# The third layer's first loads on GpSimd's queue, the offsets' filters first, and the attention's pools in another order

## The chip, the cores and the metric

The kernel runs on one core of one Trainium2 chip. A core has five engines that each work through their own list of instructions in order and wait for each other by semaphores: TensorE (PE in the profile, its weight loads PEld), VectorE (DVE), ScalarE (ACT), GpSimd (POOL) and SyncE (SP), which here only issues loads and stores. The metric is the time of one execution on the device in microseconds, as the median of several runs.

## The reference

The network takes `x` of shape (2, 256, 64, 64), two images of 256 channels, and puts four layers behind each other, all in float32:

- Layer 0: group norm, then attention with 4 heads of 64 channels over the 4096 pixels, a projection, and the normalized input added.
- Layer 1: a position term (a linear function of the pixel's row and column) is added.
- Layer 2: a bottleneck. A 1x1 convolution to 64 channels, a deformable 3x3 convolution with a mask, a 1x1 convolution back to 256, batch norms and the input added.
- Layer 3: twice group norm, ReLU and a deformable 3x3 convolution on 256 channels, and the input added at the end.

The part that matters here is the deformable convolution of layer 3:

```python
f = lax.conv_general_dilated(x, dw, (1, 1), 'SAME', feature_group_count=C, dimension_numbers=dn)
off = lax.conv_general_dilated(f, pw, (1, 1), 'SAME', dimension_numbers=dn)
off = (off + pwb[None, :, None, None]) * OFFSET_SCALE
...
sampled = bilinear_gather(x, py, px)
out = jnp.einsum('bckhw,ock->bohw', sampled, w.reshape(O, C, KK))
```

`dw` is a 7x7 filter per channel, `pw` a 1x1 convolution to 18 channels (nine taps, two coordinates). Each output pixel reads the image at nine shifted places by bilinear interpolation, four pixels for each, and the nine samples are multiplied with `w`.

## The kernel before

`Net.run` calls `attention` (layers 0 and 1, and as background work most of layer 2) and then `deform` (what is left of layer 2, and layer 3). In both, PE, ACT, DVE and POOL are put under `manual_schedule`, and SP is left out of it. What counts for this document is the order in which the instructions stand on each engine in the built program.

**Attention** goes through four units (two images, two pairs of heads), each with 16 blocks of 256 queries. For a block, PE makes scores (L533), DVE takes the largest (L542), ACT the exponentials (L549), PE turns them (L561), ACT and DVE copy them out (L576, L578), and PE multiplies with the values into `av` (L588). When a block is done, `weights` and `spread` send the softmax shares through a small table in device memory (L464) and back as `f` (L468). `combine` multiplies and adds on POOL: `o` times `f` (L474), halves added (L475), and the result written to `avs` (L480). Every second block, `project` multiplies `avs` with `wproj` on PE (L498), and DVE adds it to `res` (L508). `res` goes to device memory (L510), and `second_layer` makes the first 1x1 convolution of layer 2 from it (L840).

**Layer 2** has a class of its own, `Bottleneck`. After L840, ACT writes `h` (L850), PE transposes it (L865), DVE copies it to `imgt` (L869), and SP stores it as an image in device memory (L874). `offsets` of this class makes the offsets on PE (L883, L904), and `corners` turns them into row numbers `bidx` and weights on DVE (L671 to L709). `conv` gathers `bfour` tiles from the stored image by indirect DMA on POOL (L766), two gathers to a tile; DVE multiplies them with the weights and adds them (L947, L956, L957: `bsmp`), and PE multiplies on (L967, L976). In `deform`, `conv` of the second image uses a ring of nine `bfour` tiles (the call is `bott.pools(inner, 9)`), gathers eight tiles ahead, and is stepped along beside layer 3.

**Layer 3**, in `deform`, starts with loads on SP: four pieces of 1 MB of the first image `x` from `xn` (L1113), where the background of attention put it long before, nine tiles `wc` of the convolution's weights (L1145), and `dw` and `pw` of the offsets (L1124, L1126). DVE multiplies `dw` and `pw` into the combined filter `wf` (L1131). For each of 8 blocks of 512 pixels, 14 products on PE make `pd` from `x` and `wf` (L726; each is two records in the profile), ACT copies it to `wide` (L737), PE sums shifted copies (L743), ACT adds the bias (L752), PE transposes (L757) and `corners` makes `didx` and the weights. The main loop then gathers `four` (L766, 128 rows of 1024 numbers), weighs the four corners on ACT (L1239) and DVE (L1245) into `smp`, transposes on PE (L1257), copies to `st` on ACT (L1266) and multiplies with `wc` (L1276). `Side` objects step other work along at a fixed rate per pass: the offsets of the coming blocks, the rest of layer 2, and the images of the next layer. Ahead of the main loop, 58 passes (L1337 and on) step only the first offsets and, every third time, layer 2's `conv`.

**Places in memory.** Tiles lie in pools, and pools are stacked in the order in which they are opened. When `attention` ends, its pools are given up, and `deform`'s pools take the same places from the start on. The first instruction that writes into a pool of `deform` waits for all earlier readers and writers of the places that this pool covers. Before, attention opens `att_w`, `att_work`, `att_one`, `att_x`, `att_q`, `att_k`, `att_v`, `att_e`, `att_et` in this order; `att_one` holds `o`, `f`, `avs`, `res` and `pos`. `deform` first opens `df_w`, which holds `x` of the first image (32 KB of each partition), `dw`, `pw`, `wf`, `wide` and `wc`.

Of the kernel before, what the change touches and what calls it, by code (L numbers as in the profile page):

```python
# [9 lines left out]
F32 = mybir.dt.float32  # L10
# [8 lines left out]
P = 128  # L19
B, C, H, W = 2, 256, 64, 64  # L20
# [5 lines left out]
DWK = 7  # L26
# [12 lines left out]
class Net:  # L39
# [108 lines left out]
    def attention(self, bott):  # L148
# [4 lines left out]
        tc, nc, a = self.tc, self.nc, self.a  # L153
        with ExitStack() as ctx:
            wp = ctx.enter_context(tc.tile_pool(name="att_w", bufs=1))
            work = ctx.enter_context(tc.tile_pool(name="att_work", bufs=2))
            one = ctx.enter_context(tc.tile_pool(name="att_one", bufs=1))
            xp = ctx.enter_context(tc.tile_pool(name="att_x", bufs=4))
            qp = ctx.enter_context(tc.tile_pool(name="att_q", bufs=2))
            kp = ctx.enter_context(tc.tile_pool(name="att_k", bufs=5))  # L160
            vp = ctx.enter_context(tc.tile_pool(name="att_v", bufs=6))
            ep = ctx.enter_context(tc.tile_pool(name="att_e", bufs=4))
            etp = ctx.enter_context(tc.tile_pool(name="att_et", bufs=2))
            bt = bott.pools(ctx)
            psc = ctx.enter_context(tc.tile_pool(name="att_sc", bufs=2, space=PSUM))
            ptp = ctx.enter_context(tc.tile_pool(name="att_tt", bufs=2, space=PSUM))
# [30 lines left out]
            for i in range(NB):  # L197
                t = xp.tile([P, 2, 512], F32, name="xb") if i < 4 else rest[:, i - 4]
# [8 lines left out]
            gmask = wp.tile([P, P], F32, name="gmask")  # L207
            nc.sync.dma_start(gmask, a["gmask"][:, 0, :])
            nc.sync.dma_start(wqkv, a["wqkv"])
            wproj = wp.tile([P, 2, C], F32, name="wproj")  # L210
            self.later.append((wproj, a["wproj"]))

            units = [(b, hp) for b in range(B) for hp in range(2)]
# [407 lines left out]
            n = 0  # L621
# [453 lines left out]
    def deform(self, bott):  # L1075
# [4 lines left out]
        tc, nc, a = self.tc, self.nc, self.a  # L1080
        with ExitStack() as ctx:
            wp = ctx.enter_context(tc.tile_pool(name="df_w", bufs=1))
            work = ctx.enter_context(tc.tile_pool(name="df_work", bufs=2))
# [22 lines left out]
            x, stats = {}, dict(bott.stats)  # L1106

            def load(b, src, pool):
                x[b] = pool.tile([P, 2, HW], F32, name=f"x{b}")
                src = src.rearrange("(cb p) n -> p cb n", p=P)  # L1110
                for i in range(4):
                    cols = slice(1024 * i, 1024 * i + 1024)
                    nc.sync.dma_start(x[b][:, :, cols], src[:, :, cols])  # L1113

            load(0, self.xn_d[0], wp)
            ods = [wp.tile([P, 8, W + DWK - 1], F32, name=f"wide{n}") for n in range(2)]
            for t in ods:
                nc.gpsimd.memset(t, 0.0)
            base = bott.base

            def offset_weights(l):

                dw = wp.tile([P, 2, T], F32, name="dw")
                nc.sync.dma_start(dw, a["dw"][l])  # L1124
                pw = wp.tile([P, 2, 2 * K2], F32, name="pw")
                nc.sync.dma_start(pw, a["pw"][l])  # L1126
                yield
                yield
                self.wf = wp.tile([P, 2, T, 2 * K2], F32, name="wf")
                for cb in range(2):  # L1130
                    nc.vector.tensor_tensor(  # L1131
                        self.wf[:, cb],
                        dw[:, cb].unsqueeze(2).to_broadcast([P, T, 2 * K2]),
                        pw[:, cb].unsqueeze(1).to_broadcast([P, T, 2 * K2]),
                        ALU.mult,
                    )
                    yield
# [9 lines left out]
            def image(b, l):  # L1147

                if l == 0:
                    load(b, self.x2d[b], ctx.enter_context(tc.tile_pool(name="df_x1", bufs=1)))  # L1150
# [39 lines left out]
            def offsets(b, l):  # L1190
                if b == 0:
                    yield from offset_weights(l)
                wf = self.wf
                for i in range(NB):
                    idx = cp.tile([P, 4, K2], I32, name="didx")
                    w4 = cp.tile([P, 4, K2, 4], F32, name="dw4")
                    corners[b, l, i] = idx, w4
                    yield from self.offsets(
                        i,
                        [x[b][:, cb, :] for cb in range(2)],  # L1200
                        lambda s, row: wf[:, s, DWK * row : DWK * row + DWK, :].rearrange(
                            "p t o -> p (t o)"
                        ),
                        self.vec[:, V_PWB + l : V_PWB + l + 1],
                        base, idx, w4, work, ods, pd,
                    )

            layers = [(b, l) for l in range(2) for b in range(B)]
            BLOCK = 4 * K2
            LAYER, ALL = NB * BLOCK, len(layers) * NB * BLOCK  # L1210
            AHEAD, LEAD = 8, BLOCK + 16
# [119 lines left out]
            OFFS = 24  # L1331
            inner = ExitStack()
            second = bott.conv(1, bott.pools(inner, 9), ps)
            offs = [Side(-LEAD - 6, OFFS / BLOCK, offsets(0, 0))]
            for k in range(K2):
                conv_weight(0, k)
            for s in range(-LEAD - 6, 0):  # L1337
# [10 lines left out]
            for s in range(ALL + 12):  # L1348
                n = s // LAYER
# [22 lines left out]
                if s % LAYER == LAYER - LEAD - 8 and n + 1 < len(layers):  # L1372
                    for o in images + offs:
                        for _ in o.steps or ():
                            pass
                    images, offs = [], []
                    offs.append(Side(s, OFFS / BLOCK, offsets(*layers[n + 1])))
# [97 lines left out]
```

## Time and profile before

| what | value |
|---|---|
| median of 3 timed runs | 5586.81 us (5586.36 to 5594.37) |
| the profiled execution | 5402.33 us |
| its span, first to last instruction | 5400.6 us |
| mean granted clock of TensorE | 0.967 |
| PE, DVE, ACT, POOL busy | 92%, 79%, 54%, 38% of the span |
| last `av` product of attention ends | 3136.7 us |
| first product of the third layer's offsets | 3182.0 us |
| first `four` gather of the third layer | 3212.4 us |

The profile is one execution, recorded by the hardware; it was 184.5 us shorter than the median of the timed runs. A line of a chain gives the start, the length in microseconds, and the piece of work that the next one waited for. A line of a timeline gives start, length, engine, source line, operation, what it writes and reads, how often, and in brackets how long its engine sat idle before and what ended that. A line of the stretches gives, for each engine, the busy time and the number of instructions, then the granted clock of TensorE as a share of full speed, the share of time that the 16 DMA engines were busy, and GB/s. Records of SP and of loads are times of issue; when a load has landed is told by what waited for it.

### The profile page before, as it was taken

To read this page: it belongs to the slowest core of one execution; us is meant where nothing else is said; L and a number is where in the kernel's file an instruction comes from. 1 tells how busy PE (TensorE), PEld (TensorE's weight loads), DVE (VectorE), ACT (ScalarE), POOL (GpSimd) and SP (SyncE) were. 2 spreads that over 40 slices of the span, in tenths; PEclk is the share of its full clock that TensorE was granted. 3 is DMA by queue.
4 is the path that set the end of the run, shared out by engine and by line. 5 is a ranking of instruction groups with operands and counts; after the bars stand their busy time and mean duration, and the time that the engine had idled before them with its cause. 6 is when DMAs were issued, how large, how long until landed. Compare 5 with 4: busy or idle time off the path is not lost.

```text
span 5400.6 us, 97530 instructions
## 1 busy us (share of the span) xinstructions
PE 4976.3 (92%) x37208; PEld 2665.3 (49%) x37208; DVE 4249.0 (79%) x8066; ACT 2897.7 (54%) x5333; POOL 2068.6 (38%) x1946
## 2 busy tenths in 40 slices
PE   8999999999999999999999977767899999999998
PEld 5555555555555555555555533333444444444443
DVE  6877767787668888677766648787899999999998
ACT  5676656666566666566666622222444444444444
POOL 0111101000024343233200047777566566656665
PEclk9999999999999999999999978888999999999999
DMA  5221111101113222222141146666999999999998
GB/s 168 62 89 58 41 64 39 48 29 44 48 54 89 77 82 90 80 78 74 50 136 34 35 156 231 225 223 231 353 333 330 341 360 358 352 390 353 342 349 320
DMA packets 347363, 920.29 MB, mean 170 GB/s; under 512 B 58972, under 2 KB 98698, under 8 KB 346894
## 3 DMA queue, kind: packets, MB, share of 16 engines
q0 software_dynamic: 193536, 679.59, 35.4%
q1 hardware_dynamic: 153358, 234.46, 13.5%
q8 instruction: 292, 4.78, 0.4%
q14 instruction: 177, 1.45, 0.1%
HBM read 815.90 MB, written 89.60 MB: 168 GB/s over the span
## 4 chain that ended last, share of the span: by engine, by line
PE 65%; DVE 17%; issue 6%; DMA 5%; ACT 5%; POOL 2%; SPq 0%; ACTq 0%; DVEq 0%; POOLq 0%
PE sc L533 14%; PE av L588 14%; PE out L1276 10%; PE tt L561 9%; DVE smp L1245 8%; PE pd L726 5%; DMA four<-img,didx 3%; PE pt L1257 3%; DVE low L542 2%; ACT e L549 2%; PE pm L976 1%; POOL bfour L766 1%; DVE bfour L947 1%; PE pm L498 1%; PE pm L247 1%
## 5 line engine op out<-in xcount | busy, mean ns | idle before, releaser
L1245 DVE SCALAR_TENSOR_TENSOR smp<-four,dw,smp 128x256 f32<-128x256 f32 x3456 | 1611.8, 483 | 168.5 <-ACT smp L1239 85.5
L549 ACT ACTIVATE e<-sc,low 128x1024 f32<-128x1024 f32 x1024 | 1147.5, 1121 | 646.0 <-DVE low L542 645.0
L542 DVE TENSOR_REDUCE low<-sc 128x1 f32<-128x1024 f32 x1024 | 1209.5, 1219 | 295.9 <-PE sc L533 288.2
L766 POOL DMA_INDIRECT four<-img,didx x1152 | 1161.5, 1008 | 656.8 <-DVE smp L1245 307.7
L1276 PE MATMUL out<-st,wc 128*128 128x512 f32 x2304 | 1236.8, 619 | 139.7 <-ACT st L1266 111.3
L533 PE MATMUL sc<-k,qs 64*128 64x512 f32 x2048 | 1029.0, 621 | 7.4 <-ACT e L549 7.1
L533 PE MATMUL sc<-k,q 64*128 64x512 f32 x2048 | 1018.7, 620 | 0.0
L588 PE MATMUL av<-et,v 128*64 128x256 f32 x8192 | 999.1, 386 | 0.0
L561 PEld LDWEIGHTS tt<-ident,e 64*128 64x128 f32 x16384 | 647.9, 140 | 559.1 <-issue 245.0
L474 POOL TENSOR_TENSOR o<-o,f 128x1024 f32<-128x1024 f32 x64 | 153.4, 2396 | 1967.1 <-DVE o L428 1182.8
L766 POOL DMA_INDIRECT bfour<-img,bidx x576 | 579.8, 1007 | 665.6 <-DVE bsmp L957 487.3
L561 PE MATMUL tt<-ident,e 64*128 64x64 f32 x16384 | 751.2, 228 | 86.5 <-ACT et L578 69.4
L578 ACT COPY et<-tt 128x512 f32<-128x512 f32 x1280 | 722.2, 587 | 83.7 <-PE tt L561 80.6
L1239 ACT ACTIVATE smp<-four,dw 128x256 f32<-128x256 f32 x1152 | 524.2, 503 | 430.6 <-DMA four<-img,didx 368.9
L576 DVE COPY et<-tt 128x512 f32<-128x512 f32 x768 | 524.6, 683 | 247.3 <-PE tt L561 245.8
L1257 PEld LDWEIGHTS pt<-ident,smp 128*128 128x128 f32 x2304 | 321.1, 144 | 740.7 <-issue 439.1
L1266 ACT COPY st<-pt 128x1024 f32<-128x1024 f32 x288 | 291.0, 1010 | 721.2 <-PE pt L1257 721.2
L588 PEld LDWEIGHTS av<-et,v 128*64 128x64 f32 x8192 | 544.8, 137 | 257.0 <-issue 1.3
L1276 PEld LDWEIGHTS out<-st,wc 128*128 128x128 f32 x2304 | 393.3, 197 | 402.2 <-issue 207.1
L1257 PE MATMUL pt<-ident,smp 128*128 128x128 f32 x2304 | 457.7, 281 | 67.0 <-DVE smp L1245 61.7
L726 PE MATMUL pd<-x,wf 128*126 128x512 f32 (+2 forms) x896 | 460.8, 601 | 8.4 <-DVE wf L1131 7.3
L533 PEld LDWEIGHTS sc<-k,qs 64*128 64x128 f32 x2048 | 351.2, 192 | 229.7 <-issue 123.6
(153 smaller groups left out, 3369.1 us busy)
## 6 DMA issues: line engine op xcount, KB each, us to landing
f<-share_d SPq DMA_DIRECT2D x128, 256.0 KB, 3.9
xb<-xn SPq DMA_DIRECT2D x55, 512.0 KB, 4.0
img<-imgt SPq DMA_DIRECT2D x96, 256.0 KB, 7.0
four<-img,didx POOLq DMA_INDIRECT x1152, 6.1
xa<-res SPq DMA_DIRECT2D x32, 512.0 KB, 2.7
xb<-in_x SPq DMA_DIRECT2D x20, 512.0 KB, 5.4
bfour<-img,bidx POOLq DMA_INDIRECT x576, 3.0
qs<-q SPq DMA_DIRECT2D x64, 128.0 KB, 4.0
```

What stands on the lines that cost most here:

```text
L533: nc.tensor.matmul(s[:, j, :], lhsT=q[u, i // 2][int(h != j)][halves[j], at : at + P], rhs=k[u][c][halves[j], h, :], start=True, stop=True,)
L542: nc.vector.tensor_reduce(low, s, AX.X, ALU.max, negate=True)
L549: nc.scalar.activation(e.rearrange("p j n -> p (j n)"), s, AF.Exp, bias=blk.low[:, g, c : c + 1], accum_out=blk.sum[:, g, c : c + 1],)
L561: nc.tensor.transpose(pt[:, m, :], e[half, m // 4, m % 4 * P : m % 4 * P + P], self.ident[half, half],)
L576: nc.vector.tensor_copy(dst, pt)
L578: nc.scalar.copy(dst, pt)
L588: nc.tensor.matmul(now["av"][halves[h], :], lhsT=v[u][c][:, m, halves[h]], rhs=ets[j][:, m, h, :], start=(m == 0), stop=(m == 7),)
L726: nc.tensor.matmul(pd[:m, r0 * W : r1 * W], lhsT=wt(s, t), rhs=src[:, (y + r0) * W : (y + r1) * W], start=(n == 0), stop=(n == len(srcs) * ...
L766: self.nc.gpsimd.indirect_dma_start(out=dst, out_offset=None, in_=img, in_offset=bass.IndirectOffsetOnAxis(ap=idx, axis=0),)
L1245: nc.vector.scalar_tensor_tensor(smps[s], four[:, c], weight(s, c), smps[s], ALU.mult, ALU.add)
L1257: nc.tensor.transpose(pts[u][:, c, j * P : (j + 1) * P], smp[:, c * P : c * P + P], self.ident,)
L1276: nc.tensor.matmul(outs[ob], lhsT=wc[k][:, c, ob * P : ob * P + P], rhs=sts[u][:, c, :], start=(k == 0 and c == 0), stop=(k == K2 - 1 and ...
```

## The change

Three things are edited. In `attention`, the pools `att_work` and `att_one` are opened after `att_et` instead of after `att_w`, and `wproj` moves from `att_w` to `att_one`. In `deform`, `dw` and `pw` of the first layer and all pieces of the first image's `x` are issued on GpSimd's queue instead of SP's; those of the second layer and of the second image stay on SP. And the generator of the first offsets is made and stepped once ahead of the load of `x`, so that `dw` and `pw` are issued first; the same generator is handed on to the `Side` that steps it later.

```diff
--- before.py
+++ after.py
@@ -153,14 +153,15 @@
         tc, nc, a = self.tc, self.nc, self.a
         with ExitStack() as ctx:
             wp = ctx.enter_context(tc.tile_pool(name="att_w", bufs=1))
-            work = ctx.enter_context(tc.tile_pool(name="att_work", bufs=2))
-            one = ctx.enter_context(tc.tile_pool(name="att_one", bufs=1))
             xp = ctx.enter_context(tc.tile_pool(name="att_x", bufs=4))
             qp = ctx.enter_context(tc.tile_pool(name="att_q", bufs=2))
             kp = ctx.enter_context(tc.tile_pool(name="att_k", bufs=5))
             vp = ctx.enter_context(tc.tile_pool(name="att_v", bufs=6))
             ep = ctx.enter_context(tc.tile_pool(name="att_e", bufs=4))
             etp = ctx.enter_context(tc.tile_pool(name="att_et", bufs=2))
+
+            work = ctx.enter_context(tc.tile_pool(name="att_work", bufs=2))
+            one = ctx.enter_context(tc.tile_pool(name="att_one", bufs=1))
             bt = bott.pools(ctx)
             psc = ctx.enter_context(tc.tile_pool(name="att_sc", bufs=2, space=PSUM))
             ptp = ctx.enter_context(tc.tile_pool(name="att_tt", bufs=2, space=PSUM))
@@ -207,7 +208,7 @@
             gmask = wp.tile([P, P], F32, name="gmask")
             nc.sync.dma_start(gmask, a["gmask"][:, 0, :])
             nc.sync.dma_start(wqkv, a["wqkv"])
-            wproj = wp.tile([P, 2, C], F32, name="wproj")
+            wproj = one.tile([P, 2, C], F32, name="wproj")
             self.later.append((wproj, a["wproj"]))
 
             units = [(b, hp) for b in range(B) for hp in range(2)]
@@ -1110,20 +1111,18 @@
                 src = src.rearrange("(cb p) n -> p cb n", p=P)
                 for i in range(4):
                     cols = slice(1024 * i, 1024 * i + 1024)
-                    nc.sync.dma_start(x[b][:, :, cols], src[:, :, cols])
-
-            load(0, self.xn_d[0], wp)
-            ods = [wp.tile([P, 8, W + DWK - 1], F32, name=f"wide{n}") for n in range(2)]
-            for t in ods:
-                nc.gpsimd.memset(t, 0.0)
+                    queue = (nc.gpsimd, nc.sync)[b]
+                    queue.dma_start(x[b][:, :, cols], src[:, :, cols])
+
             base = bott.base
 
             def offset_weights(l):
 
+                queue = (nc.gpsimd, nc.sync)[l]
                 dw = wp.tile([P, 2, T], F32, name="dw")
-                nc.sync.dma_start(dw, a["dw"][l])
+                queue.dma_start(dw, a["dw"][l])
                 pw = wp.tile([P, 2, 2 * K2], F32, name="pw")
-                nc.sync.dma_start(pw, a["pw"][l])
+                queue.dma_start(pw, a["pw"][l])
                 yield
                 yield
                 self.wf = wp.tile([P, 2, T, 2 * K2], F32, name="wf")
@@ -1205,6 +1204,13 @@
                         base, idx, w4, work, ods, pd,
                     )
 
+            begun = offsets(0, 0)
+            next(begun)
+            load(0, self.xn_d[0], wp)
+            ods = [wp.tile([P, 8, W + DWK - 1], F32, name=f"wide{n}") for n in range(2)]
+            for t in ods:
+                nc.gpsimd.memset(t, 0.0)
+
             layers = [(b, l) for l in range(2) for b in range(B)]
             BLOCK = 4 * K2
             LAYER, ALL = NB * BLOCK, len(layers) * NB * BLOCK
@@ -1331,7 +1337,7 @@
             OFFS = 24
             inner = ExitStack()
             second = bott.conv(1, bott.pools(inner, 9), ps)
-            offs = [Side(-LEAD - 6, OFFS / BLOCK, offsets(0, 0))]
+            offs = [Side(-LEAD - 6, OFFS / BLOCK, begun)]
             for k in range(K2):
                 conv_weight(0, k)
             for s in range(-LEAD - 6, 0):
```

## The prediction

> **What bounds the kernel now.** I read the page's chain shares first, then the chain in order of time, and looked for where attention ends and the deformable layer begins, since every edit lies there. This is the chain around that place, not its whole length; the columns are start, length (us) and what.
>
> ```profile
> 3149.38 3.69 PE pm L840 x4
> ...
> 3161.71 12.27 DMA wc<-in_dcw
> 3173.98 0.02 issue
> 3174.00 6.83 DMA pw<-in_pw
> 3180.83 0.03 DVEq L1131
> 3180.86 0.04 issue
> 3180.91 1.09 DVE wf L1131
> 3182.00 0.04 issue
> 3182.04 12.90 PE pd L726 x28
> ```
>
> The first product of the offsets (`pd`) starts at 3182.04 because `wf` needs `dw` and `pw`, and SP issued those last, behind four megabytes of `x` and nine `wc`. Next, busy time per stage (PE, PEld, DVE, ACT, POOL, then granted clock, DMA share, GB/s):
>
> ```profile
> 3137.00:3182.00 45.00, 22.96 (x40) 8.83 (x40) 10.42 (x46) 5.58 (x10) 21.36 (x22) 0.55 0.70 245
> 3182.00:3213.00 31.00, 26.92 (x78) 12.32 (x78) 10.44 (x32) 1.87 (x3) 12.88 (x13) 0.94 0.20 59
> ```
>
> For 45 us PE is half idle at half clock; then for 31 us it is busy while POOL waits and DMA idles. Two phases that could overlap stand one after the other. The timeline of POOL shows which wait ends last (start, length, what, idle before and its releaser):
>
> ```profile
> 3139.14 2.34 POOL L474 TENSOR_TENSOR o<-o,f 128x1024 f32<-128x1024 f32 x1 [37.56 <-DMA f<-share_d]
> ...
> 3161.15 0.99 POOL L766 DMA_INDIRECT bfour<-img,bidx  x1 [6.02 <-issue]
> ...
> 3186.09 0.94 POOL L766 DMA_INDIRECT bfour<-img,bidx  x1 [0.30 <-issue]
> 3201.14 0.94 POOL L766 DMA_INDIRECT bfour<-img,bidx  x1 [14.11 <-DVE floor L685]
> ...
> 3212.38 0.94 POOL L766 DMA_INDIRECT four<-img,didx  x1 [0.30 <-issue]
> ```
>
> POOL issues 28 gathers of the second layer, then the first `four`, which opens the third layer's loop. After 20 it stands for 14.11 us: the ring of nine `bfour` tiles is full, and the sums that free it stand on DVE behind `pos<-pd`, which waits for `pd`. So the loop's start is set by the image store (first gather 3161.15) plus 51.2 us of gathers, of which about 15 are a stall that goes back to late `dw` and `pw`. Everything later runs in order behind this.
>
> **What the Trainium skill says.** "DMA: Bandwidth & Descriptors", section "Issuing engines are not separate DMA queues": loads from GpSimd and from SP share the same 16 engines, so moving issues saves sequencer time only. The trace agrees so far as gathers and SP's loads together reach 406 GB/s at 3162 to 3168. Same page, "Anatomy of one DMA — SWDGE (gpsimd) path": about 2.0 us plus bytes/436 GB/s, 4.4 us for 1 MB; no plain load from GpSimd is in this trace. "TensorE: Matmul & The Clock Gate", "What's actually happening": half clock after some 3.4 us idle, full after 3.4 us of work. The trace agrees: granted 1.00 at 3120 to 3137, 0.50 from 3144 to 3182, 1.00 from 3190.
>
> **The change, part by part.** In the changed program's order on each engine, read from the built code:
>
> (a) The pools' order. Before, `df_w` lay over `att_work` and `att_one`, so its first tile waited for the last reader of `res`, the L840 product (3153.06). After, it lies over `att_w`, `att_x`, `att_q`, `att_k` and part of `att_v`, and the wait of `dw` is for the last `av` product (L588), which ends at 3136.7. Head start 16 us. `wproj` moves to `att_one` since L498 reads it late. Within attention only addresses differ and the order is the same: nothing.
>
> (b) POOL now has `dw`, `pw`, `x` piece 1 ahead of the last L474, piece 2 ahead of L475, piece 3 ahead of L480, piece 4 after it. The issue cost of a plain load on POOL is not in this trace. Lower bound SP's 0.37 us (L1113); the nearest POOL row is a gather, 0.95 us plus 0.30 gap for 128 rows; a piece of `x` has 256 runs, so up to twice that. I take 1.0 for `dw` and `pw`, 1.3 for a piece, each plus 0.3. Then `dw` 3136.8, `pw` 3138.1, piece 1 3139.4 to 3140.7, L474 3141.0 instead of 3139.14, and with 1.6 each for two more pieces `avs` is ready at 3149.1 instead of 3143.6: 5.5 us later.
>
> (c) SP, freed of `x`, issues the nine `wc` right after 3136.7 (4 MB less ahead of them). They share the engines with piece 1. At the trace's 380 GB/s some 1.2 of their 2.36 MB are through at 3140.7; sharing alike, piece 1 is in after another 2 MB, 5.3 us, and about 1 us until it counts as landed (an estimate, half of that page's fixed 2.0): 3147. `wf` needs `dw` and `pw` (about 3 us after issue, as a `bfour` gather) and 2.1 us on DVE: 3144, hidden by piece 1. SP then holds the second layer's `dw` until `wf` is done; behind it stand `res`, `xa` and the image store, none of which is due before 3157, so that wait costs nothing (with `wf` later than 3157 it would).
>
> (d) On PE six `pd` products now stand ahead of the first L498, and the other eight between L498, L840, L865 and L883. So attention's tail waits for piece 1: this is what is late next. From 3147: fourteen products took 12.90 us, of which about 2.2 are the cold start (warm, 512 columns take 2 x 0.43). Six are 4.5 warm plus 2.2: 3153.7, when `avs` is long there. But PE is now warm. L498 takes about 1.0 instead of 2.07, L840 1.9 instead of 3.67, and single `pd` fill the waits for DVE (0.70) and ACT (1.08). Stepping through: L498 3153.7, L498 3155.6, L840 3157.4, L865 3160.4, `imgt` copied 3161.4. It was 3155.4: 6.0 us later.
>
> (e) The image store was issued over 2.6 us and the gather followed 3.8 us after the last issue began, with DMA 0.98 busy by `x`. After, `x` and `wc` (6.4 MB from 3137.6 at 380 GB/s) are through by 3155, and the short store's usual landing is 2.2 us, so the first gather comes at 3165.8: 4.6 later than 3161.15.
>
> (f) The 14.11 us stall goes. The remaining `pd` end at about 3168, `pos<-pd` comes at about 3180, and the tile that the 21st gather needs is freed by 3184, while that gather is due at 3191. 28 gathers at 1.25 are 35 us, plus about 2 for those that run beside DVE's sums (1.4 each at 3201 to 3212): 37 instead of 51.2, a gain of 14.2. The memsets of `wide` (1.07 us) stay ahead of the gathers and stay hidden.
>
> Sum: 14.2 - 4.6 = 9.6 us earlier first `four`. Later, the offset products stand one place earlier in the first loop: nothing, PE is 0.72 busy there. Against the profiled execution (5402.33 us, span 5400.6) this is 5392.7. The three timed runs have a median of 5586.81, 184.5 longer; the page does not say where, so I take the same microseconds off: 5577.2. A measurement of this kernel can tell about 0.2%, 11.2 us, from no change.
>
> **Rivals.**
> 1. Cheaper on POOL: a plain load holds POOL no longer than SP, 0.37 us. Piece 1 is issued at 3137.8, lands about 3144.5, and everything from (d) on comes 2.5 us earlier; if the warm PE also saves on the second L883 and L904, the delay is 1 to 2 us and the gain 12 to 14: 5573.5. For: the granted clock of 0.50 through the whole old tail. Against: every POOL DMA in the trace costs 0.95.
> 2. Slower: the tail waits too long for piece 1. The price is one for one from 14.2 us of delay on, and plus 0.2% needs 25.4, so piece 1 landing at about 3168 instead of 3147. The place is the six `pd` ahead of L498 on PE. For: a `wc` under a full queue took 12.27 us to land. Against: even 12.27 us gives 3153 and leaves a gain of 3.6; it would take POOL standing several us on each megabyte. About 5598.
> 3. Given back: the gain is there at 3213, but the loop later loses it. From 3900 on DMA is 0.94 to 0.95 busy at about 349 GB/s, and if what limits there were not the start but heat or another clock state, the end would hardly move: 5586. Against: all of that work is behind the same gathers and starts as much earlier.
> That the loads aren't earlier at all is excluded by the waits in (a).
>
> **How the numbers follow.** The sum as worked out, gain 6 to 11: 0.42. Rival 1: 0.43, since several of my terms are taken high and the ring's stall is fully removed in each case. Rival 3: 0.07. Rival 2: 0.08. Hence faster 0.43, same 0.49, slower 0.08. The predicted time is the sum's, 5577. Its own range is 5575 to 5582 with the unknown POOL issue (gain 5 to 12). For 8 in 10: down to a gain of 17 (no delay of the tail and the spread of the three runs, 8 us, halved), up to a loss of 3: 5570 to 5590.
>
> **What would show it.** Right: `dw` issued by POOL at 3137; `wf` before 3146; the first `pd` before L498, near 3147; L498 near 3154 at about 1 us; first gather at 3164 to 3167; no idle above 2 us between the 28 gathers; first `four` near 3203, and the same distance to the end from there. Wrong: plain loads on POOL of several us; piece 1 after 3152; `imgt` after 3166; a stall of POOL on a `bfour` tile; or a distance from first `four` to the end that differs from 2188 us by more than 3.

## The result, and the profile after

| | before | after |
|---|---|---|
| median of 12 timed runs each | 5587.62 us (5575.4 to 5604.42) | 5581.61 us (5567.48 to 5603.61) |
| ratio, with 95% interval | | 0.9979 [0.9966, 0.9993] |
| the profiled execution, and its span | 5402.33, 5400.6 us | 5603.61, 5601.8 us |
| last `av` product ends | 3136.72 us | 3166.63 us |
| first `four` gather, after that | 75.7 us | 70.0 us |
| from there to the end | 2188.2 us | 2365.2 us |

The kernel is shorter by 6.0 us by the medians, and by 11.7 us (0.21%) by the recorded ratio, which isn't the quotient of the two medians (0.9989); its interval reaches from 0.07 to 0.34%, to both sides of what was named as distinguishable.

The two profiled executions can't be compared as wholes: the kernel before took 5408 us in some sessions and 5588 us in others, once each on chip 14, and the profile of before is of the first kind, that of after of the second. So I count from the end of the last `av` product. Source lines of the changed kernel stand from one lower to six higher (L474 is L475, L498 is L499, L726 is L727, L766 is L767, L1131 is L1130).

The timeline of POOL after answers to the one shown of before (start, length, what, in brackets the idle time before it and what ended it):

```profile
3167.27 0.60 POOL L1123 DMA_DIRECT2D dw<-in_dw  x1 [35.79 <-PE av L589]
...
3168.41 0.74 POOL L1115 DMA_DIRECT2D x<-xn  x1
3169.46 2.33 POOL L475 TENSOR_TENSOR o<-o,f 128x1024 f32<-128x1024 f32 x1 [0.32 <-DMA f<-share_d]
...
3196.59 1.03 POOL L767 DMA_INDIRECT bfour<-img,bidx  x1 [19.24 <-DMA img<-imgt]
...
3228.67 1.15 POOL L767 DMA_INDIRECT bfour<-img,bidx  x1 [4.31 <-DVE bsmp L958]
...
3236.66 0.94 POOL L767 DMA_INDIRECT four<-img,didx  x1 [0.30 <-issue]
```

The loads come straight after the `av` product; the first gather comes 30.0 us after it (24.4 before); and the stall of 14.11 us is a stall of 4.31. PE after, where the chain of before showed `pd` as the last of all:

```profile
3176.45 7.34 PE L727 MATMUL pd<-x,wf 128*126 128x512 f32 x12 [9.82 <-DMA x<-xn]
3183.63 1.02 PE L499 MATMUL pm<-avs,wproj 128*128 128x512 f32 x2
...
3187.34 1.93 PE L841 MATMUL pm<-res,w 128*64 128x512 f32 x4
```

`pd` starts 9.8 us after the last `av` product instead of 45.3, and now attention's tail stands behind it. The stretches (busy us of PE, PEld, DVE, ACT, POOL, then granted clock, DMA share, GB/s), first up to the gathers, then the gathers:

```profile
3166.00:3197.00 31.00, 21.18 (x51) 8.74 (x48) 5.36 (x6) 3.08 (x5) 10.14 (x12) 0.83 0.81 274
3197.00:3237.00 40.00, 24.39 (x76) 10.78 (x74) 15.37 (x71) 4.36 (x8) 27.46 (x29) 0.83 0.38 115
```

Before, it was 45 us at a clock of 0.55 and 31 at 0.94; now PE is busy for 0.68 and 0.61 of the two stretches, at 0.83 in both. What is left of the stall stands behind waits of DVE for which this profile has no releaser ("remote"). Over the whole execution there are 68 such waits of 451 us, nearly all on ACT and DVE, and none in the profile of before:

```profile
3207.99 0.23 DVE L672 TENSOR_TENSOR pos<-pm,base 128x72 f32<-128x72 f32 x1 [4.78 <-remote]
...
3212.23 0.23 DVE L672 TENSOR_TENSOR pos<-pd,base 128x72 f32<-128x72 f32 x1 [3.54 <-remote]
```

### The profile page after: what moved, and what is told of

Its sections match the earlier page's. It is cut to its first block, busy times and chain, and to the rows that moved or that the text cites. A ratio compares the mean times of both kernels' runs of the same rounds, so it can differ in the third digit from the quotient of the medians.

```text
span 5601.8 us, 97517 instructions
## 1 busy us (share of the span) xinstructions
PE 5000.3 (89%) x37208; PEld 2671.1 (48%) x37208; DVE 4247.3 (76%) x8066; ACT 2883.7 (51%) x5333; POOL 2062.6 (37%) x1952
## 5 line engine op out<-in xcount | busy, mean ns | idle before, releaser
L767 POOL DMA_INDIRECT four<-img,didx x1152 | 1153.9, 1002 | 765.5 <-DVE smp L1251 337.8
L475 POOL TENSOR_TENSOR o<-o,f 128x1024 f32<-128x1024 f32 x64 | 153.5, 2399 | 1939.4 <-DVE o L429 1154.3
L767 POOL DMA_INDIRECT bfour<-img,bidx x576 | 577.1, 1002 | 766.3 <-DVE bsmp L958 583.9
L1245 ACT ACTIVATE smp<-four,dw 128x256 f32<-128x256 f32 x1152 | 511.2, 502 | 55.5 <-DMA four<-img,didx 45.9
L727 PE MATMUL pd<-x,wf 128*126 128x512 f32 (+2 forms) x896 | 467.3, 608 | 16.1 <-DMA x<-xn 9.8
```

Of the source, the lines that this page charges most:

```text
L727: nc.tensor.matmul(pd[:m, r0 * W : r1 * W], lhsT=wt(s, t), rhs=src[:, (y + r0) * W : (y + r1) * W], start=(n == 0), stop=(n == len(srcs) * ...
L767: self.nc.gpsimd.indirect_dma_start(out=dst, out_offset=None, in_=img, in_offset=bass.IndirectOffsetOnAxis(ap=idx, axis=0),)
```

## The experiments

My theory is the prediction's: `dw` and `pw`, last in SP's queue, made the stall, and the tail pays a part back by waiting for the first piece of `x`. (The run with the pools' order alone corrects its first half.) The rivals tested: that one part of the change alone gives it, that the queue gives it, that the end doesn't follow the start. "Head" is the time from the end of the last `av` product to the first `four` gather, "rest" from there to the end, both in one profiled execution; "gain" is the difference of the two medians in the same session.

| run | median (before) us | ratio [95%] | gain us | head us | rest us |
|---|---|---|---|---|---|
| e0, before again | 5408.42 (5407.65) | 1.0004 [0.9996, 1.0013] | -0.8 | 75.7 | 2194.6 |
| e1, after again | 5395.14 (5407.65) | 0.9977 [0.9968, 0.9985] | 12.5 | 65.3 | 2189.9 |
| e4, all on SP | 5388.08 (5407.65) | 0.9969 [0.9957, 0.9981] | 19.6 | 59.3 | 2193.6 |
| e6, ring of 11 | 5399.9 (5407.65) | 0.9986 [0.9979, 0.9992] | 7.8 | 71.4 | 2190.7 |
| e2, pools only | 5398.27 (5407.12) | 0.9985 [0.9979, 0.9992] | 8.9 | 74.6 | 2185.8 |
| e3, queue only | 5400.26 (5407.12) | 0.9987 [0.998, 0.9993] | 6.9 | 68.1 | 2194.1 |
| e5, `x` on SP | 5385.58 (5407.12) | 0.9961 [0.9947, 0.9974] | 21.5 | 59.8 | 2189.2 |
| e7, fewer ahead | 5390.67 (5407.12) | 0.9964 [0.9951, 0.9978] | 16.5 | 46.3 | 2203.6 |
| e10, pools only again | 5579.21 (5587.61) | 0.9989 [0.9981, 0.9997] | 8.4 | 75.2 | 2343.3 |
| e11, `x` on SP again | 5570.71 (5587.28) | 0.9958 [0.9945, 0.9972] | 16.6 | 67.3 | 2351.7 |

### Both kernels again, in one session

No edit in e0 (the kernel before) and e1 (the changed kernel).

> The kernel before, unchanged, for a second profile of it. The way from the last av product of attention to the first four gather took 75.7 us in the profile before and 70.0 in the profile after. Theory (the start of the third layer's loop is the image store plus 28 gathers, with a stall of some 14 us on the ring of bfour tiles): 75 to 76 us again, and a stall of 13 to 15 us on POOL in it. Rival (the two profiles differ by the state of the chip and not by the edit): the way varies by several us from one execution to the next, 70 to 80. The span shows as well whether 5400.6 us was an unusual execution: near 5590 if so.

> The changed kernel, unchanged, for a second profile and a narrower interval. Theory: 66 us from the last av product to the first four gather where no engine waits for something that the profile does not show, up to 70 where it does as in the profile after; 8 to 12 us less than before in the timed runs, ratio 0.998. Rival (a gain in the stage that the loop gives back): the same 66 to 70, but a ratio of 1.000.

Neither profile has a "remote" wait, so these two can be compared. The head fell from 75.7 to 65.3 us, 10.4 less; the median by 12.5. Chain of e1 in order of time (start, length, what):

```profile
3142.00 7.59 DMA x<-xn
3149.59 0.14 issue
3149.73 6.87 PE pd L727 x12
3156.60 0.86 PE pm L499 x2
...
3160.22 1.86 PE pm L841 x4
...
3163.89 0.44 DVE imgt L870
...
3166.33 2.21 DMA img<-imgt
```

This is step (d): piece 1 of `x`, six `pd`, then L499, L841 and the image store. The gathers of e1 on POOL:

```profile
3169.41 1.03 POOL L767 DMA_INDIRECT bfour<-img,bidx  x1 [18.82 <-DMA img<-imgt]
...
3205.56 0.94 POOL L767 DMA_INDIRECT four<-img,didx  x1 [0.30 <-issue]
```

28 gathers in 36.2 us, and none of them waits for more than 0.31 us. The rest is 2189.9 us; the unchanged kernel alone showed 2188.2 and 2194.6. So nothing above that scatter was given back.

### The stall by itself: a larger ring

```diff
-            self.ahead = gathers - 1
+            self.ahead = min(gathers - 1, 8)
...
-            second = bott.conv(1, bott.pools(inner, 9), ps)
+            second = bott.conv(1, bott.pools(inner, 11), ps)
```

> The kernel before with a ring of eleven bfour tiles instead of nine in the third layer, still eight tiles ahead; no load is moved. Theory (the stall on the ring sets the loop's start): four more gathers run before the stall, which shrinks by 5 us, so 70 to 71 us from the last av product to the first four gather, and about 5 us less in time. Rival (the late pd product sets it in another way, through didx): the first four stays where it is, 75 to 76 us.

Nothing else of the kernel before is touched; two more tiles take four more gathers before POOL stands. POOL of e6:

```profile
3199.03 0.95 POOL L766 DMA_INDIRECT bfour<-img,bidx  x1 [10.03 <-DVE floor L685]
...
3205.12 1.08 POOL L766 DMA_INDIRECT four<-img,didx  x1 [0.30 <-issue]
```

The stall is 10.0 instead of 14.0 us, the head 4.3 us shorter, the median 7.8 (interval 4.3 to 11.4). The stall on the ring is on the path to the end: less of it, by another means and with all loads as late as before, shortens the kernel. That the median fell by more than the head isn't explained by this, though its interval takes in 4.3.

### The pools' order alone

```diff
-            work = ctx.enter_context(tc.tile_pool(name="att_work", bufs=2))
-            one = ctx.enter_context(tc.tile_pool(name="att_one", bufs=1))
...
+            work = ctx.enter_context(tc.tile_pool(name="att_work", bufs=2))
+            one = ctx.enter_context(tc.tile_pool(name="att_one", bufs=1))
...
-            wproj = wp.tile([P, 2, C], F32, name="wproj")
+            wproj = one.tile([P, 2, C], F32, name="wproj")
```

> Only the pools' order and the place of wproj are changed; all loads stay on SP in the old order (x, then wc, then dw and pw). Times counted from the end of the last av product, beside 17.6 (x), 45.5 (first pd) and 75.7 us (first four gather) of the kernel before. Theory (dw and pw set the start, wherever x stands): x is issued at 0 to 1 us, but dw and pw still stand behind nine wc, so the first pd comes at 30 to 40; the first pos<-pd moves forward by as much, the stall of POOL on the bfour ring shrinks from 14 to about 7 us, and the first four gather comes at 68 to 70: about 7 us less in all. Rival A (the early x is the gain): first four at 60 to 65, 11 us or more. Rival B (early x without early filters is worth nothing): first four at 75 to 76, within 2 us of before.

The head is 74.6 us, rival B. My number for `pd` was wrong (30 to 40; it came at 43.2). This is SP's queue in e2:

```profile
3136.14 1.41 SPq L1114 DMA_DIRECT2D x<-xn  x3
3148.87 0.36 SPq L511 DMA_DIRECT2D xa<-res  x1
3149.27 0.47 SPq L1114 DMA_DIRECT2D x<-xn  x1
...
3157.56 4.91 SPq L1146 DMA_DIRECT2D wc<-in_dcw  x9
3162.51 0.51 SPq L1125 DMA_DIRECT2D dw<-in_dw  x1
```

Three pieces of `x` go at once, but the fourth stands behind the store of `res` in SP's own order, and `dw` behind `wc`, 26.4 us after the last `av` product. That is 10 us earlier than in e0 (36.5), yet `wf` came only 2 us earlier. DVE tells why; first e2, then the kernel before:

```profile
3177.76 0.54 DVE L710 TENSOR_TENSOR bw<-wt 128x36 f32<-128x36 f32 x4
3178.19 2.06 DVE L1132 TENSOR_TENSOR wf<-dw,pw 128x882 f32<-128x882 f32 x2
```

```profile
3178.37 0.54 DVE L709 TENSOR_TENSOR bw<-wt 128x36 f32<-128x36 f32 x4
3180.91 2.07 DVE L1131 TENSOR_TENSOR wf<-dw,pw 128x882 f32<-128x882 f32 x2 [2.00 <-DMA pw<-in_pw]
```

In both, `wf` stands on DVE behind `corners` of the second layer (`bw`), which waits for attention's tail. In e2 `wf` follows it with no idle time: it waited for its place on DVE and for no load, and a stall of 13.89 us stayed. In the kernel before it waited for `pw` only 2.00 us longer. So filters that land earlier are by themselves worth about these 2 us. The rest of the gain goes with the place of `wf`: in the runs that issue the filters first (e1, e3, e4, e5) the built program has it ahead of `corners`, and it starts 2.7 to 21.1 us after the last `av` product instead of 42.1. No run moves `wf` on DVE alone.

Yet the median was 8.9 us less, where the head gives 1.1. Repeated in another session:

> The kernel with the pools' order alone once more, unchanged. If its 8.9 us were scatter, it is now 0 to 4 us less than the kernel before (the first four gather 1.1 us earlier); if they are real, again 6 to 11 us less. In the trace the first four gather should again stand at 74 to 75 us after the last av product, and POOL should again stall for 13.5 to 14.2 us on the bfour ring.

Again 8.4 us less, with a head of 75.2 us and POOL standing for 2.03 and 12.95 us among the gathers. So it isn't scatter of one session, and it doesn't come from the head.

### Attention by itself

In both kernels the call of the deformable part is replaced by a constant that fills the output:

```diff
-            self.deform(bott)
+            for b in range(B):
+                for cb in range(2):
+                    for i in range(HW // P):
+                        dst = self.out[b, P * cb : P * cb + P, P * i : P * i + P]
+                        self.nc.sync.dma_start(dst, self.ident)
```

> The kernel before without its deformable part: after attention the output is filled with a constant, so that only attention and its tail are timed. With its partner below this asks whether the pools' order alters attention itself, since the kernel with the pools' order alone was timed 8.9 us shorter where its trace shows the first four gather only 1.1 us earlier. Theory 1 (attention is the same, the 8.9 us are scatter or lie after attention): the two medians agree within 2 us. Theory 2 (other addresses make attention shorter): the partner is 4 to 8 us shorter.

> The kernel with the pools' order alone, cut in the same way after attention. Theory 1: within 2 us of its partner with the old order. Theory 2: 4 to 8 us shorter.

With the old order 3221.36 us (3215.47 to 3227.69, five runs), with the new one 3217.31 (3210.03 to 3218.91): 4.05 us less by the medians, at a granted clock of 0.976 and 0.979 on average. The ranges overlap, so this doesn't settle theory 2. The two kernels aren't attention alone either: SP issued the 128 stores of the constant in the midst of the first blocks (71 to 147 us), and at 128 us PE sat idle for 13.2 us in e8 and 15.9 us in e9 while they ran. And the profiles of the whole kernel speak against theory 2: in those without a "remote" wait the last `av` product ends at 3133.7 to 3139.3 us with the old order (before, e0, e3, e6) and at 3127.6 to 3142.7 us with the new one (e1, e2, e4, e5, e7), with means of 3136.6 and 3136.3. Between e0 and e2 most of the difference stands in the rest, which differs by 6.4 us between two profiles of the unchanged kernel. So the 8.9 and 8.4 us were timed twice, and where they come from is open.

### The queue and the loads' order alone

The pools stay as before; the edits of `deform` are those of the changed kernel.

```diff
-                    nc.sync.dma_start(x[b][:, :, cols], src[:, :, cols])
+                    queue = (nc.gpsimd, nc.sync)[b]
+                    queue.dma_start(x[b][:, :, cols], src[:, :, cols])
...
+            begun = offsets(0, 0)
+            next(begun)
+            load(0, self.xn_d[0], wp)
```

> Only the queue and the order of the loads are changed (dw, pw, then x of the first half from GpSimd); the pools stay as before, so all of them wait for the last product of L840, some 16 us after the last av product. Theory (the filters' order alone gives most of the gain): wf at about 22 us after the last av product, the first pd at about 34, pos<-pd at about 54, the stall of POOL 5 us or less, first four at 65 to 67: about 9 us less in all, nearly that of the whole change, since attention's tail no longer waits for x. Rival (the pools' order is what gives the gain): first four at 75 to 76, within 2 us of before. A third outcome: the loads stand on GpSimd ahead of the first bfour gathers, which come later by their wait (5 us or more), and the gain falls to 4 us or less.

The head is 68.1 us, 7.6 less: near the theory's 9, with a part of the third outcome. The new order of the loads does remove the stall (no gap above 0.5 us among the gathers), though they start 18.2 us late: `wf` stands on DVE ahead of `corners`, which begins with `pos<-pm`.

```profile
3160.34 2.06 DVE L1129 TENSOR_TENSOR wf<-dw,pw 128x882 f32<-128x882 f32 x2 [2.36 <-DMA img<-imgt]
3165.87 0.23 DVE L671 TENSOR_TENSOR pos<-pm,base 128x72 f32<-128x72 f32 x1 [3.46 <-PE pm L904]
```

But POOL of e3 shows what it costs:

```profile
3157.41 0.60 POOL L1122 DMA_DIRECT2D dw<-in_dw  x1 [10.95 <-ACT h L850]
...
3158.56 2.83 POOL L1114 DMA_DIRECT2D x<-xn  x4
...
3171.52 1.04 POOL L766 DMA_INDIRECT bfour<-img,bidx  x1 [9.05 <-issue]
```

The image stores were issued at 18.8 us as before, but the first gather comes at 32.3 instead of 24.8: four megabytes of `x` and the `wc` were issued from 17.6 us on, just around the stores. (That they share the DMA engines with the stores is my reading of this; it wasn't tried by itself.) The pools' order (1.1 us of head) and the queue with the filters first (7.6) give together 10.4, and not their sum of 8.7. As I read the traces, an early `x` has no use while `wf` stands late, and late loads collide with the image.

### The same with other queues

e4 is the changed kernel with every load on SP, in the new order; e5 has `dw` and `pw` on GpSimd and only `x` on SP.

```diff
-                    queue = (nc.gpsimd, nc.sync)[b]
+                    queue = nc.sync
                     queue.dma_start(x[b][:, :, cols], src[:, :, cols])
...
-                queue = (nc.gpsimd, nc.sync)[l]
+                queue = nc.sync
                 dw = wp.tile([P, 2, T], F32, name="dw")
```

> The pools' order and the filters ahead of all stay, but dw, pw and x go on SP's queue again. On PE only one pd product then stands between the two L498, not six ahead of the first. Theory (the queue is not what gains; it even costs, by putting the first piece of x behind wc and six products ahead of L498): the first pd near 8 us after the last av product, the image store 5 us earlier than in the changed kernel, 61 to 63 us from the last av product to the first four gather, some 14 us less than before, ratio 0.9970 to 0.9980. Rival (GpSimd's queue is what makes the loads early): near the kernel before, 73 to 76 us and a ratio of 1.000.

> The whole change, but the four pieces of x are issued by SP; dw and pw stay on GpSimd. The whole change gave the first four gather at 65.3 us after the last av product, the same with all loads on SP 59.3. Theory (the 6 us between the two come from x on GpSimd: its issues stand ahead of o<-o and avs, and its pieces share the DMA engines with the wc that SP issues at the same time): first four at 59 to 61, first L499 product at 8 to 10, 5 us less than the whole change. Rival (it is dw and pw on GpSimd, or the queue as such): first four at 64 to 66, L499 at 16.

e4 has a head of 59.3 us (61 to 63 expected) and e5 of 59.8, against 65.3 of the change. So GpSimd's queue isn't needed, and it is `x` on it that costs 5.5 us. The issues themselves (0.74 us each) are a small part: `avs` is ready at 8.6 us in e1 and at 7.3 in e5. PE of e5 tells the order:

```profile
3142.13 2.07 PE L499 MATMUL pm<-avs,wproj 128*128 128x512 f32 x2 [7.37 <-POOL avs L481]
3144.00 1.91 PE L727 MATMUL pd<-x,wf 128*126 128x512 f32 x2
3145.70 1.25 PE L499 MATMUL pm<-avs,wproj 128*128 128x512 f32 x2
```

With `x` on SP the built program has L499 ahead of the first `pd`, as soon as `avs` is there (7.4 us); with `x` on GpSimd six `pd` stand ahead of L499, and attention's tail waits for piece 1 of `x` (16.2 us), 7.6 us after `avs` is ready. The first gather then comes at 23.2 instead of 29.2. So most of what the change gave back went to an order of PE, as the traces have it; no run has `x` on GpSimd and L499 first. e5 has the lowest median of all whole kernels, and it was repeated:

> The kernel with x on SP and only dw and pw on GpSimd once more, since its 21.5 us rest on five runs. Theory (the head's 15.9 us and the pools' order are both real): again 14 to 24 us less than the kernel before, ratio 0.9957 to 0.9974, the first four gather at 59 to 62 us after the last av product with no stall of POOL above 2 us. Rival (a good part was scatter): 8 to 13 us less, near the whole change's 12.5.

Again 0.9958 [0.9945, 0.9972], 16.6 us by the medians: the theory's band. But the head was 67.3 us, outside its 59 to 62, and POOL stalled for 8.56 us. ACT stood before `od` (L753), which `pos<-pd` waits for by way of PE; first e11, then the same instruction in e5:

```profile
3209.09 0.69 ACT L753 ACTIVATE od<-pd,vec 128x512 f32<-128x512 f32 x1 [14.17 <-remote]
```

```profile
3170.39 0.69 ACT L753 ACTIVATE od<-pd,vec 128x512 f32<-128x512 f32 x1 [2.06 <-PE pd L744]
```

The same program waits 14.17 us where it waited 2.06. The products that `od` reads (L744) are recorded as ended at 3198.6 us, 10.5 us before it starts, and the profile doesn't say what came between.

### Fewer gathers ahead of the loop

e7 is e4 with one more edit, for a shorter kernel still.

```diff
-                if s % 3 == 0:
+                if s % 6 == 0:
                     next(second)
```

> As the kernel with all loads on SP and the filters first, but of the second layer only every sixth step in place of every third is taken ahead of the third layer's loop: about 18 bfour gathers in place of 28 stand ahead of the first four gather, the others follow inside the loop. Theory (the gathers ahead of the loop are on the path, and inside the loop GpSimd, busy 73% there, has room for ten more): first four at 46 to 50 us after the last av product in place of 59.3, the distance from there to the end grows by less than 12 us, and the time is 2 to 12 us less than with all loads on SP. Rival (the loop is bound by GpSimd or by what the second layer delivers at its end, and gives it all back): the distance grows by 12 us or more, no gain over that kernel (ratio to the kernel before 0.997 or above).

18 gathers stand ahead of the loop instead of 28:

```profile
3166.28 0.99 POOL L767 DMA_INDIRECT bfour<-img,bidx  x1 [15.09 <-DMA img<-imgt]
...
3189.06 0.95 POOL L767 DMA_INDIRECT four<-img,didx  x1 [0.31 <-issue]
```

The head falls by 13.0 us against e4, to 46.3, as the theory had it; but the rest grows by 10.0 to 2203.6 (2193.6 in e4, 2185.8 to 2194.6 in all others without a "remote" wait). The gain is 16.5 us against 19.6 by the medians, and by the ratios 0.9964 against 0.9969, in two sessions. So of the 2 to 12 us that the theory expected over e4 nothing is clear of noise: most of what the ten gathers cost ahead of the loop, they cost inside it.

## Why the prediction was right

The predicted 5577 us stands beside 5581.61 measured, inside the sum's own range of 5575 to 5582; 9.6 us were expected, and 6.0 (medians), 11.7 (ratio) and, in e1, 12.5 were found.

The forecast of the stage came true, but its account of the kernel before was too simple. "`wf` needs `dw` and `pw`, and SP issued those last" is worth 2.00 us there, by the trace of before and by e2; for the rest `wf` was late because of its place on DVE. The sum still came out, since its times for `wf` and `pd` follow the order of the changed program, in which that place is another.

Step by step, in us after the last `av` product:

| step | predicted | e1 | profile after |
|---|---|---|---|
| first load issued (a) | 0.1 | 0.6 | 0.6 |
| L475 starts (b) | 4.3 | 2.7 | 2.8 |
| `wf` ready (c) | 7.3 | 9.5 | 8.4 |
| first `pd` (c) | 10.3 | 9.5 | 9.8 |
| L499 (d) | 17.0 | 16.2 | 17.0 |
| L841 (d) | 20.7 | 19.9 | 20.7 |
| first `bfour` gather (e) | 29.1 | 29.2 | 30.0 |
| first `four` gather (f) | 66.1 | 65.3 | 70.0 |

**(a)** The wait is for the last `av` product, as read. "Within attention only addresses differ: nothing" isn't contradicted by the profiles, in which attention ends no earlier; but e2 and e10 were timed 8.9 and 8.4 us shorter with a head shorter by 1.1 and 0.5, so the pools' order is worth something that the prediction put at nothing.

**(b)** was mis-sized: 1.0 and 1.3 us of issue with 0.3 us of gap, where 0.57 to 0.60 and 0.72 to 0.76 without a gap were measured; `avs` is ready at 8.6 us, not 12.4 (the terms given add up to 5.1 us of delay and not 5.5, so 12.0). It didn't matter, because L499 waits for piece 1 and not for `avs`. That also answers rival 1: its price, 0.37 us, is too low and mine was too high, and the gain of the head stayed at 10.4, under its 12 to 14. The 12.5 us timed in e1 lie in that band, but not by its way.

**(c)** was right for piece 1: it is issued 0.9 us earlier than I had it (1.8 instead of 2.7) and takes 7.59 us from the start of its issue until it counts, where I had 7.6. Meanwhile, from 3142.0 to 3149.6 us, the DMA share is 1.04, at 356 GB/s, which agrees with sharing the DMA engines with `wc`. Of rival 2's landing at 31 us nothing was seen. `wf` was mis-sized: its two operations took 3.98 us on DVE in e1 and 3.13 in the profile after, not 2.1. I called it hidden by piece 1 with 3 us to spare; in e1 it was ready at 9.5 us, level with the piece at 9.4, so this cover was used up.

**(d), (e)** The six `pd` took 6.87 us (6.7 predicted), the warm L499 1.02 and L841 1.93. That 3.4 us of work bring back the full clock is too short a rule for this trace: in the kernel before PE was busy for 5.43 us in one stretch (L883, 3155.4 to 3160.9 us) and the clock stayed at 0.50. Here it did come back in time. The delay of the tail was real. What I didn't see is that it was an order that the queue of `x` brings with it: e5 has the same loads without the six products ahead.

**(f)** The stall is gone in e1, and 28 gathers take 36.2 us where 37 was predicted. In the profile after, 4.31 us of stall come back by waits of DVE that I had no reason to expect.

**Rival 3**, given back later, finds no support: the rest of e1 lies within the scatter of the kernel before. But the sign that I named for it, a distance that differs from 2188 us by more than 3, was too narrow: the unchanged kernel gave 2194.6. And in the profile after it is 2365.2 us, as it is long in the other two profiles with "remote" waits (2343.3 in e10, where only the pools' order is changed, and 2351.7 in e11); there is no such profile of the kernel before beside them.

So the stage went as predicted, with the one correction above. That the timed gain fits as well is in part luck: the sum has nothing in it for the pools' order, which alone was timed at 8.4 us beside a kernel before of 5588 us, where the whole change was timed at 6.0 to 11.7. The runs can't separate the two in the change itself. That the loads' part is real in time as well is shown by e5 and e2 in one session, whose intervals don't meet (0.9947 to 0.9974, and 0.9979 to 0.9992).

## What to carry to other kernels

When a small load is last in its queue, look at what stands behind it and not only at the bytes, and look at where its reader stands on its own engine. Here the start of a 2190 us stage hung on one product of two small filters, by way of a ring of gather tiles. Filters issued 10 us earlier moved it by 2 us as long as the built program had it behind another layer's work on DVE; issuing them ahead of all else, on either queue, came with another place on DVE and took the stall away. Freeing the memory earlier gave 1.1 us of head by itself, and it was timed at some 8 us more that no trace explains. And after moving a load to another queue, compare the order on the compute engines too: here the move put six products ahead of the tail, and took back 5.5 of 15.9 us.

## What the runs showed of the hardware that was not expected

- A plain load issued by GpSimd held it for 0.57 to 0.60 us (`dw`, `pw`) and 0.72 to 0.76 us (1 MB of `x`), less than an indirect gather (0.95 us and 0.30 us until the next).
- Three profiles of the whole kernel have waits named "remote": 68 of them with 451 us in the profile after, 42 with 295 us in e10, 62 with 396 us in e11. These three have spans of 5574 to 5602 us; the nine without such waits have 5380 to 5407. What the waits are for is open.
- The unchanged kernel's distance from the first `four` gather to the end differed by 6.4 us between two profiles without such waits, so that a single profile of each kernel can't show less than that over a long stage.
